# Two-level Strassen kernel on one core: DVE takes the sums, ten more products are split, two small constants are recorded later

## The chip, the cores and the metric

The kernel runs on 1 core of one Trainium2 chip. The metric is the device time of one execution in microseconds. Of the engines, PE is the matrix engine (PEld its weight load), DVE the vector engine, ACT the scalar engine, POOL the GpSimd engine, and SP the queue that issues most of the DMA transfers. Engines run their own instruction streams in order and wait for each other by semaphores.

## The reference

```python
x = x + einsum('bnr,bor->bno', einsum('bni,bri->bnr', x, B0[ids0]), A0[ids0])   # rank-16 adapter by request
base   = einsum('btd,od->bto', x, W)
logits = einsum('btd,ed->bte', x, Wr) + 5.0 * one_hot(ids1, 8)[:, None, :]
topw, topi = top_k(logits, 2); gates = sum(one_hot(topi, 8) * softmax(topw)[..., None], axis=-2)
h = einsum('btd,erd->bter', x, A1)
x = x + base + 2.0 * einsum('bter,bte,eor->bto', h, gates, B1)                  # 8 experts of rank 16
```

x is 64 x 64 x 1024 in float32, so 4096 tokens of 1024; W is 1024 x 1024. All of it is float32.

## The kernel before

The tokens lie transposed and are cut into 8 blocks of 512. Each block's first part (`early`) turns the gathered rows of the first adapter on PE (`turn`, tile pt, from a tile gb that POOL gathers by an indirect DMA), projects x by them (`project`, tile pb<-x,bt), and adds the adapter's output to x (`adapt`, tile px). The second part (`late`) computes the router's logits and the 128 expert rows (`rows`, tile ph), the gates by a chain of small DVE instructions (`gates`), and turns the gated rows on PE (`weigh`, tile pg). Two blocks make one of 4 super-blocks.

The large matrix product, W with the identity added times x, is done by super-block in two nested levels of a 7-product scheme (Strassen's in Winograd's form). The outer level makes 7 outer products (order 1, 2, 6, 7, 5, 3, 4), each on sums of quarters of W and of the tokens. Inside each, 7 inner products are made from smaller quarters, again in the order 1, 2, 6, 7, 5, 3, 4. An inner product multiplies a 128 x 512 weight tile (tag s) with a 128 x 512 token tile (ti, or a view of x or t) into PSUM tiles pa and pb: 4 matmuls that are 256 columns wide, and 2 more for the expert part's bias rows where there is one. Super-block 0 makes the sums of the weights and stores them to DRAM (`s_kept`); the later ones load them again. Outer product 1 of super-block 0 is made whole (tile pw).

From super-block 1 on, some inner products are split by a third level (`fine_product`, tile pf): 7 matmuls that are 128 columns wide take the place of the 4. Their operands are four extra sums of the weight tile (`fine_weights`, tile sf, made in super-block 1, kept in `f_kept`, loaded later) and four of the token tile (`begin_fine`, tile tt). The first four matmuls fill PSUM, and the last three, interleaved with other products, add to it, while ACT copies the half-done parts out (tile cp) and later instructions add them to the result. Which products are split is set by `fine_of`: product 2 of every outer product, and product 4 of those in `FOURTH`.

Vector work between the levels: `token_sum` (t), `inner_tokens` (ti), `outer` and `weights` (s, by `combine`), the evictions from PSUM with an addition (`leave`) and the sums of outputs (`done`). In super-block 0 `inner_tokens` is DVE's, later POOL's; the sums in `weights`, `fine_weights`, `begin_fine` and the additions of cp (`rest_`) are POOL's.

The order is not that of the source. Every step is handed to `Plan.add` with the engines it may run on, their cost in us, what it reads and writes, the pool slots it takes and a due time `at`. `Plan.order` simulates the engines with these costs: it picks the engine that can start first, and on it the step with the earliest due time among those that can start within 0.2 us. An argument `behind` holds a step back until another has begun in the plan. The instructions are then recorded in the planned order, and a scheduling layer adds the semaphores. `PACE` slows two steps that the plan puts on DVE and POOL at the same time. `SET` is when the engines are ready at the start. Every instruction is recorded through the helper at line 29, so all have one line in the profile and are told apart by their tiles. The mask that the projection's result is multiplied with, and a float copy of the experts' order, are made on DVE in front of the plan (lines 311 and 312).

Of the kernel before, what the change touches and what calls it, by code (L numbers as in the profile page):

```python
# [14 lines left out]
P = 128  # L15
# [18 lines left out]
class Plan:  # L34
# [15 lines left out]
    PACE = {"DVE": 0.36, "POOL": 0.73}  # L50
    SET = {"SP": 1.2, "DVE": 3.1, "POOL": 2.9}
# [13 lines left out]
    def order(self):  # L65
# [35 lines left out]
        clock, end, where, now = dict(self.SET), {}, {}, {}  # L101
        moved = 0.0
# [5 lines left out]
        def start(n, e):  # L108
# [20 lines left out]
            return t  # L129

        while ready:
# [8 lines left out]
            t0 = min(can[e])[0]  # L140
            _, n, t = min((steps[n]["at"], n, t) for t, n in can[e] if t <= t0 + self.LOOK)
# [3 lines left out]
            other = {"DVE": "POOL", "POOL": "DVE"}.get(e)  # L145
            if st["sb"] and other in now and clock[other] > t and steps[now[other]]["sb"]:

                mine, theirs = st["eng"][e] / self.PACE[e], (clock[other] - t) / self.PACE[other]
                both = min(mine, theirs)
                clock[e] = t + both + (mine - both) * self.PACE[e]  # L150
                clock[other] = t + both + (theirs - both) * self.PACE[other]
                end[now[other]] = clock[other]
            now[e] = n
# [28 lines left out]
def kernel(  # L182
# [74 lines left out]
    FOURTH = (1, 2, 6, 7, 3)  # L257
# [6 lines left out]
        "q": 7, "s": 27, "tt": 3, "cp": 3, "t5": 2, "t6": 2, "t7": 2, "t4": 2, "o": 3, "hg": 3, "hd": 3,  # L264
# [46 lines left out]
    dve.tensor_scalar(mask, mask, half, None, ALU.is_equal)  # L311
    dve.tensor_copy(order, order_i)
    b1_sb = const.tile([P, O], F32, name="b1_sb")

    def consts():
# [9 lines left out]

        plan.add({"POOL": 0.2}, hold, [(("gb", 0),)], [("a1",)], -56)
# [8 lines left out]
    def biases():  # L335
# [19 lines left out]
        plan.add({"DVE": 1.0}, languages, [("ids1",)] + whole(0), [("bias",)], -45)  # L355
# [47 lines left out]
    def gather(k, tag, table, at):  # L403
        def fn(e):
            made[tag, k] = new(tag, [P, D], f"{tag}_{k}")
            pool.indirect_dma_start(
                out=made[tag, k],
                out_offset=None,
                in_=table,
                in_offset=bass.IndirectOffsetOnAxis(ap=idx[:, k : k + 1], axis=0),  # L410
            )

        plan.add(
            {"POOL": 1.1}, fn, [], [((tag, k),)], at, [(tag, (tag, k))], kb=512,
            behind=[(("x", 0, 1), 0, 0)] * ((tag, k) == ("ga", 0)) + [("a1",)] * (k == 1) + [(("px", 1, 1, 0),)] * (k > 1),
        )
# [22 lines left out]
    def project(k, at):  # L439
# [29 lines left out]
        plan.add({"DVE": 0.3}, out, [(pb,)], [(bx,)], at - 8)  # L469

    def adapt(k, h, at):
# [33 lines left out]
        for gi in range(NG):  # L505
            xs = part(x, gs=[gi])
            plan.add({"DVE": 0.62}, out(gi), [(px[gi],)] + xs, xs, at - 2 + 1.5 * gi * (k == 0))
# [159 lines left out]
    f_kept = tc.dram_tile([7, 2, P, QC * QO], F32, name="f_kept")  # L667

    def fine_of(s, n):

        return ((2, 4) if n in FOURTH and (s, n) != (NSUP - 1, ORDER[-1]) else (2,)) if s >= FINE else ()
# [13 lines left out]
    DVE = {"DVE": 0.62}  # L685
    POOL = {"POOL": 1.25}

    def outer(n, at):

        if n == 5:  # L690
            m_q[5] = {k: ("m5",) + k for k in quarter[1, 0]}
            for k in m_q[5]:
                combine(m_q[5][k], quarter[1, 0][k], quarter[1, 1][k], ALU.add, at, DVE)
        elif n == 7:
            m_q[7] = quarter[1, 0]
            for k in m_q[7]:
                combine(m_q[7][k], quarter[0, 0][k], m_q[7][k], ALU.subtract, at, DVE)
        elif n == 6:
            m_q[6] = quarter[0, 0]
            for k in m_q[6]:  # L700
                combine(m_q[6][k], m_q[5][k], m_q[6][k], ALU.subtract, at, DVE)
        elif n == 3:
            m_q[3] = quarter[0, 1]
            for k in m_q[3]:
                combine(m_q[3][k], m_q[3][k], m_q[6][k], ALU.subtract, at, DVE)
# [3 lines left out]
    def weights(s, n, at):  # L709
# [17 lines left out]
        for k, (u, v, op) in {  # L727
# [8 lines left out]
            combine(out[k], uu, vv, op, at - 4, POOL)  # L736
# [9 lines left out]
    def fine_weights(s, n, k, a, at):  # L746

        t, kept = ("sf", s, n, k), f_kept[n - 1, k // 4]

        def blocks():  # L750
            made[t] = new("s", [P, QC, QO], f"sf_{s}_{n}{k}")
            return made[t].rearrange("p c (o w) -> p (c o) w", w=P)
# [5 lines left out]
        def sums(e):  # L758
            f, w4 = blocks(), made[a].rearrange("p c (o w) -> p (c o) w", w=P)
            a11, a21, a12, a22 = (w4[:, x] for x in range(4))  # L760
            v = engine[e]
            v.tensor_tensor(f[:, 0], a21, a22, ALU.add)
            v.tensor_tensor(f[:, 1], f[:, 0], a11, ALU.subtract)
            v.tensor_tensor(f[:, 2], a11, a21, ALU.subtract)
            v.tensor_tensor(f[:, 3], a12, f[:, 1], ALU.subtract)
# [4 lines left out]
        if s == FINE:  # L770
            plan.add({"POOL": 1.6}, sums, [(a,)], [(t,)], at - 3, [("s", t)], sb=True)
            plan.add({"SP": 0.1}, keep, [(t,)], [("fine", n, k)], at + 4, kb=256)
        else:
            plan.add({"SP": 0.1}, load, [("fine", n, k)], [(t,)], at - 6, [("s", t)], kb=256)
# [25 lines left out]
    def inner_tokens(s, n, m, at):  # L800
# [7 lines left out]
        for k, u, v in ((5, (0, 1), (0, 0)), (6, (1, 1), 5), (7, (1, 1), (0, 1)), (4, (1, 0), 6)):  # L808
            t = ("ti", s, n, k)

            def fn(e, t=t, k=k, u=u, v=v):
# [6 lines left out]
                POOL if s else DVE, fn, keys(*u) + vk, [(t,)], at - 5,  # L818
# [40 lines left out]
    def products(s):  # L859
# [91 lines left out]
        def leave(n, ps, i, cs, js, more=False):  # L951
# [18 lines left out]
            if d == n and not fresh:  # L970
                reads.append((name(d, i), 0, 0))
            plan.add(
                {"ACT": 0.6} if src is None else DVE, fn, reads, qk(d, i, cs, js), at() - 4,
# [5 lines left out]
        def begin_fine(n, k):  # L979
# [3 lines left out]
            def fn(e):  # L983
                made[t] = new("tt", [P, 4, P], f"tt_{s}_{n}{k}")
                f, b, v = made[t], tx(), engine[e]
                b11, b21 = b[:, 0, :P], b[:, 1, :P]
                v.tensor_tensor(
                    f[:, :2], b[:, :, P:], b[:, 0, :].rearrange("p (h t) -> p h t", t=P), ALU.subtract
                )
                v.tensor_tensor(f[:, 2], f[:, 1], b11, ALU.add)  # L990
                v.tensor_tensor(f[:, 3], b21, f[:, 2], ALU.subtract)

# [315 lines left out]
```

## Time and profile before

| | us |
|---|---|
| median of 5 runs | 515.65 |
| lowest, highest | 515.17, 517.30 |
| the profiled execution | 515.5 |
| its span | 513.7 |
| PE, PEld busy | 499.6, 440.8 |
| DVE, POOL, ACT busy | 328.5, 319.7, 71.4 |

The profile is of one execution. Busy time of an engine is the time that its instructions cover; a record of an instruction that waits for a port that another engine holds includes that wait. Each float32 matmul leaves two PE records, and successive records overlap, so what a matmul costs PE is the distance between starts. The part of the span that no engine's work explains is seen in the waits: for each engine, what it waited for and how long. The whole program reads 75.3 MB from DRAM and writes 32.8.

### The profile page before, as it was taken

The numbers are of one execution on the slowest core, as the hardware profiler recorded it, in microseconds if no ns is written. First come the engines' busy times: TensorE is split into PE (matmuls) and PEld (weight loads), VectorE is DVE, ScalarE is ACT, GpSimd is POOL, SyncE is SP. The second block draws the span as 40 slices with busy tenths as digits, with TensorE's granted clock in tenths as the row PEclk, the third lists the DMA queues.
The fourth block names the chain that finished last, engine by engine and source line by source line (L and its number), as shares of the span: only waits on it lengthen the run. The fifth ranks groups of instructions, "written<-read, shape, count | busy, mean of one in ns | idle before, by whom it ended". The sixth has DMA issues, their size and how long they took to land.

```text
span 513.7 us, 9478 instructions
## 1 busy us (share of the span) xinstructions
PE 499.6 (97%) x3648; PEld 440.8 (86%) x3648; DVE 328.5 (64%) x589; ACT 71.4 (14%) x189; POOL 319.7 (62%) x405
## 2 busy tenths in 40 slices
PE   2999999999999999999999999999999999999997
PEld 2857988888889998899888999889889899999986
DVE  0799998987965276536985456463777526742833
ACT  1111100001001130013110221102301111111110
POOL 3072058195567686997858557972954755997811
PEclk9999999999999999999999999999999999999999
DMA  8999175799576303999577644981855754581123
GB/s 275 372 362 385 66 265 214 270 326 308 178 245 215 93 2 125 330 336 352 179 237 253 218 125 127 379 273 44 286 180 181 245 154 144 166 265 41 40 98 109
DMA packets 59452, 108.69 MB, mean 212 GB/s; under 512 B 5520, under 2 KB 11664, under 8 KB 59408
## 3 DMA queue, kind: packets, MB, share of 16 engines
q1 hardware_dynamic: 57104, 99.70, 57.6%
q0 software_dynamic: 2304, 8.39, 4.8%
q8 instruction: 29, 0.48, 0.4%
q14 instruction: 15, 0.12, 0.1%
HBM read 75.30 MB, written 32.77 MB: 210 GB/s over the span
## 4 chain that ended last, share of the span: by engine, by line
PE 97%; DMA 2%; DVE 0%; issue 0%; SPq 0%; POOL 0%
PE pa L29 39%; PE pb L29 23%; PE pf L29 15%; PE ph L29 12%; PE px L29 3%; PE pw L29 3%; DMA x<-in_xT 2%; PE pt L29 1%; PE pg L29 1%; DVE o L29 0%; SPq L29 0%; DVE bx L29 0%; POOL x L29 0%
## 5 line engine op out<-in xcount | busy, mean ns | idle before, releaser
L29 PE MATMUL pa<-ti,s 128*128 128x256 f32 x432 | 102.0, 380 | 0.0
L29 PEld LDWEIGHTS pa<-ti,s 128*128 128x128 f32 x432 | 79.2, 190 | 9.8 <-issue 0.2
L29 PE MATMUL pb<-ti,s 128*128 128x256 f32 x264 | 65.6, 380 | 0.0
L29 PE MATMUL ph<-a_sb,x 128*128 128x136 f32 x512 | 62.8, 279 | 0.2 <-issue 0.2
L29 PEld LDWEIGHTS ph<-a_sb,x 128*128 128x128 f32 x512 | 61.8, 190 | 1.1 <-issue 0.4
L29 ACT COPY cp<-pf 128x128 f32<-128x128 f32 (+1 forms) x108 | 32.2, 303 | 200.8 <-PE pf L29 188.9
L29 PEld LDWEIGHTS pb<-ti,s 128*128 128x128 f32 x264 | 48.6, 190 | 5.9
L29 PE MATMUL pa<-x,s 128*128 128x256 f32 x216 | 52.4, 380 | 0.0
L29 POOL TENSOR_TENSOR ti<-x,ti 128x512 f32<-128x512 f32 x24 | 32.0, 1334 | 27.4 <-PE pf L29 22.6
L29 POOL TENSOR_TENSOR o<-o,cp 128x128 f32<-128x128 f32 (+1 forms) x54 | 34.5, 652 | 20.8 <-DVE o L29 15.6
L29 DVE TENSOR_TENSOR x<-px,x 128x512 f32<-128x512 f32 x64 | 39.8, 681 | 10.8 <-PE px L29 10.7
L29 PEld LDWEIGHTS pa<-x,s 128*128 128x128 f32 x216 | 39.4, 190 | 4.9 <-issue 0.2
L29 PE MATMUL pf<-tt,sf 128*128 128x128 f32 x216 | 42.1, 278 | 0.0
L29 POOL TENSOR_TENSOR ti<-x 128x512 f32<-128x512 f32 x24 | 31.0, 1295 | 16.7 <-PE pb L29 11.2
L29 PE MATMUL pa<-t,s 128*128 128x256 f32 x168 | 41.2, 380 | 0.0
L29 POOL TENSOR_TENSOR ti<-t 128x512 f32<-128x512 f32 x18 | 22.9, 1273 | 29.0 <-PE pa L29 16.6
L29 PEld LDWEIGHTS pf<-tt,sf 128*128 128x128 f32 x216 | 35.5, 191 | 3.2 <-issue 0.8
L29 DVE TENSOR_TENSOR o<-pa,u 128x512 f32<-128x512 f32 x32 | 22.0, 686 | 22.3 <-PE pa L29 11.2
L29 POOL TENSOR_TENSOR s<-w,w 128x512 f32<-128x512 f32 x12 | 17.2, 1429 | 29.1 <-PE pa L29 13.2
L29 POOL TENSOR_TENSOR ti<-t,ti 128x512 f32<-128x512 f32 x18 | 25.3, 1404 | 15.7 <-PE pf L29 12.1
L29 PEld LDWEIGHTS pa<-t,s 128*128 128x128 f32 x168 | 30.8, 190 | 3.9 <-issue 0.2
L29 DVE TENSOR_TENSOR o<-pb,o 128x512 f32<-128x512 f32 x35 | 23.5, 687 | 8.9 <-ACT o L29 4.6
(150 smaller groups left out, 849.4 us busy)
## 6 DMA issues: line engine op xcount, KB each, us to landing
s<-s_kept SPq DMA_DIRECT2D x147, 256.0 KB, 4.3
x<-in_xT SPq DMA_DIRECT2D x15, 1024.0 KB, 8.7
out_T<-o SPq DMA_DIRECT2D x30, 512.0 KB, 3.0
s_kept<-s SPq DMA_DIRECT2D x28, 256.0 KB, 5.1
sf<-f_kept SPq DMA_DIRECT2D x24, 256.0 KB, 3.6
s_kept<-w SPq DMA_DIRECT2D x18, 256.0 KB, 5.3
w<-in_w SPq DMA_DIRECT2D x16, 256.0 KB, 8.2
f_kept<-sf SPq DMA_DIRECT2D x12, 256.0 KB, 2.5
```

Of the source, the lines that this page charges most:

```text
L29: return self._tc.keep_in_program_order(f(*args, **kwargs))
```

## The change

`inner_tokens`, `weights` and the additions of cp (`rest_`) become DVE's alone. `rest_` is now two instructions of 256 columns, not three of 128 and 256. The sums for the split products' operands (`begin_fine`, `fine_weights`) become steps of their own, one instruction each, that the plan may put on DVE or on POOL.

`FOURTH` takes in outer products 5 and 4, and a new `THIRD` splits product 3 of outer products 3 and 4. The last outer product of the last super-block stays with product 2 alone. The eviction of a split product 3 goes to column half 1 (`js`), and pa is evicted there after product 5.

In the planner the pacing is gone. A step that touches the port that DVE and POOL share (`sb`) starts after the last such step has ended (`shared_`). DVE's costs are 0.65 for a sum and 0.69 for an eviction.

The mask and the experts' order become a planned step behind block 0's first gather. Block 2's first gather gets a POOL copy of one column ahead of it, which waits for block 1's second half of x. The weight pool has 26 slots, not 27.

```diff
-    PACE = {"DVE": 0.36, "POOL": 0.73}
-    SET = {"SP": 1.2, "DVE": 3.1, "POOL": 2.9}
+    SET = {"SP": 1.2, "DVE": 2.6, "POOL": 2.9}
...
-            return t
+
+            return (max(t, shared_), t) if st["sb"] else (t, t)
...
-            now[e] = n
+            if st["sb"]:
+                shared_ = clock[e]
...
-    FOURTH = (1, 2, 6, 7, 3)
+    FOURTH = (1, 2, 6, 7, 5, 3, 4)
+    THIRD = (3, 4)
...
-        "q": 7, "s": 27, "tt": 3, "cp": 3, "t5": 2, "t6": 2, "t7": 2, "t4": 2, "o": 3, "hg": 3, "hd": 3,
+        "q": 7, "s": 26, "tt": 3, "cp": 3, "t5": 2, "t6": 2, "t7": 2, "t4": 2, "o": 3, "hg": 3, "hd": 3,
...
-    dve.tensor_scalar(mask, mask, half, None, ALU.is_equal)
-    dve.tensor_copy(order, order_i)
...
+        def finish(e):
+            dve.tensor_scalar(mask, mask, half, None, ALU.is_equal)
+            dve.tensor_copy(order, order_i)
+
+
+        plan.add({"DVE": 0.4}, finish, [], [("mask",), ("order",)], -57, behind=[(("gb", 0),)])
...
+        held = (tag, k) == ("gb", 2)
+
+        def hold(e):
+
+            made[tag, k] = new(tag, [P, D], f"{tag}_{k}")
+            pool.tensor_copy(made[tag, k][:, :1], made["x", 1, 1][:, 0, :1])
+
+        if held:
+            plan.add(
+                {"POOL": 0.2}, hold, part(("x", 1, 1), [0]), [((tag, k),)], at, [(tag, (tag, k))]
+            )
...
-    f_kept = tc.dram_tile([7, 2, P, QC * QO], F32, name="f_kept")
+    f_kept = tc.dram_tile([7, 3, P, QC * QO], F32, name="f_kept")
...
-        return ((2, 4) if n in FOURTH and (s, n) != (NSUP - 1, ORDER[-1]) else (2,)) if s >= FINE else ()
+        if s < FINE:
+            return ()
+        if (s, n) == (NSUP - 1, ORDER[-1]):
+            return (2,)
+        return (2,) + (4,) * (n in FOURTH) + (3,) * (n in THIRD)
...
-            combine(out[k], uu, vv, op, at - 4, POOL)
+            combine(out[k], uu, vv, op, at - 4, {"DVE": 0.65})
...
-            plan.add({"POOL": 1.6}, sums, [(a,)], [(t,)], at - 3, [("s", t)], sb=True)
+            for x in range(4):
+                plan.add(
+                    {"DVE": 0.29, "POOL": 0.48}, sums(x), [(a,)] + [(t, y) for y in range(x)], [(t, x)], at - 3,
+                    [("s", t)] * (x == 0), sb=True,
+                )
...
-                POOL if s else DVE, fn, keys(*u) + vk, [(t,)], at - 5,
+                {"DVE": 0.65} if s else DVE, fn, keys(*u) + vk, [(t,)], at - 5,
...
-            plan.add({"POOL": 1.7}, fn, tk, [(t,)], at() - 3, [("tt", t)], sb=True)
+            for x, cost in enumerate(({"DVE": 0.42, "POOL": 0.75}, {"DVE": 0.29, "POOL": 0.48}, {"DVE": 0.29, "POOL": 0.48})):
+                plan.add(
+                    cost, sums(x), tk + [(t, y) for y in range(x)], [(t, x)], at() - 3,
+                    [("tt", t)] * (x == 0), sb=True,
+                )
...
-            leave(n, ps, row, ALL, (0,), True)
-            region = qk(dest[n], row, ALL, (0,))
-
-            def rest_(e):
-                o, c, v = q(dest[n], row, ALL, (0,)), made[cp], engine[e]
-                c11, c21, c2 = o[:, 0, :P], o[:, 1, :P], o[:, 1]
-                v.tensor_tensor(c11, c11, c[:, 0], ALU.add)
-                v.tensor_tensor(c2, c2, c[:, 1:3].rearrange("p h t -> p (h t)"), ALU.add)
-                v.tensor_tensor(c21, c21, c[:, 3], ALU.add)
-
-            plan.add({"POOL": 1.7}, rest_, [(cp,)] + region, region, at() - 4, sb=True)
-            done(n, row, ALL, (0,))
+            leave(n, ps, row, ALL, js, True)
+            region = qk(dest[n], row, ALL, js)
+
+            def rest_(x):
+                def fn(e):
+                    o, c, v = q(dest[n], row, ALL, js), made[cp], engine[e]
+
+                    o, c = (o[:, :, :P], c[:, 0::3]) if x == 0 else (o[:, 1].rearrange("p (h t) -> p h t", t=P), c[:, 1:3])
+                    v.tensor_tensor(o, o, c, ALU.add)
+
+                return fn
+
+            for x in range(2):
+                plan.add({"DVE": 0.42}, rest_(x), [(cp,)] + region, region, at() - 4, sb=True)
+            done(n, row, ALL, js)
...
+                if k == 5 and 3 in fine_of(s, n):
+                    leave(n, ps, 0, ALL, (1,))
...
-                    if k == 7 and 4 in fine_of(s, n):
-                        going.append([n, 4, 0])
+                    if k in (6, 5) and k - 2 in fine_of(s, n):
+                        going.append([n, k - 2, 0])
                     advance()
-                if 4 in fine_of(s, n):
-                    rest = [(n, 3)]
-                    continue
+                rest = [(n, k) for k in (3, 4) if k not in fine_of(s, n)]
+                if last(n):
+                    rest = [(n, 4), (n, 3)]
+                continue
```

## The prediction

> **What bounds the kernel now.** I read the waits of TensorE first, then the chain that ended last, the table by stretches of time, and the instructions of PE in order of time.
>
> ```profile
> PE 499.6 (97%) x3648; PEld 440.8 (86%) x3648; DVE 328.5 (64%) x589; ACT 71.4 (14%) x189; POOL 319.7 (62%) x405
> ...
> PE 97%; DMA 2%; DVE 0%; issue 0%; SPq 0%; POOL 0%
> ```
>
> ```profile
> PE pt L29 <- DMA gb<-in_b,idx: 9.3, 1, 9.3
> PE pb L29 <- DMA x<-in_xT: 0.6, 1, 0.6
> PE px L29 <- DVE bx L29: 0.4, 1, 0.4
> PE ph L29 <- issue: 0.2, 1, 0.2
> ```
>
> The second fence is every wait that PE has: about 10.5 us, all before 18.3 us. After that PE runs to 510.1 us without a pause, and the last store lands at 513.7. So between 18 and 510 us only two things count: how long PE's own instructions take, and whether a helper becomes late enough to stop PE. The stretches show how near the helpers are to that (columns: busy us and instructions of PE, PEld, DVE, ACT, POOL, then clock, DMA share, GB/s):
>
> ```profile
> 20.00:150.00 130.00, 129.98 (x984) 108.07 (x983) 115.91 (x214) 11.32 (x24) 64.02 (x60) 1.00 0.77 267
> 150.00:273.00 123.00, 123.00 (x934) 110.62 (x933) 76.11 (x135) 20.10 (x56) 95.31 (x130) 1.00 0.61 212
> 273.00:396.00 123.00, 123.00 (x935) 110.72 (x934) 73.62 (x135) 20.00 (x56) 79.83 (x102) 1.00 0.62 201
> ```
>
> DVE is 89% busy from 20 to 150 us (super-block 0) and about 61% in each later super-block; PE stands still in neither, and its clock is 1.00 throughout.
>
> **The change part by part.** *1. Ten more split products.* In super-blocks 1 to 3, product 4 is now split for outer products 5 (three times) and 4 (twice; the very last outer product stays out), and product 3 for outer products 3 (three times) and 4 (twice): 10 products. A whole one is 4 matmuls 256 columns wide, a split one is 7 matmuls 128 wide; each matmul leaves two records. Bias matmuls stay as they are. What each costs PE is the distance between starts, since records overlap:
>
> ```profile
> 236.37 1.89 PE L29 MATMUL pa<-ti,s 128*128 128x256 f32 x8
> 238.10 0.39 PE L29 MATMUL pf<-tt,sf 128*128 128x128 f32 x2
> ...
> 245.04 0.61 PE L29 MATMUL pf<-x,s 128*128 128x128 f32 x4
> 245.49 0.39 PE L29 MATMUL pf<-tt,sf 128*128 128x128 f32 x2
> 245.71 0.39 PE L29 MATMUL pf<-tt,s 128*128 128x128 f32 x2
> 245.93 1.89 PE L29 MATMUL pa<-x,s 128*128 128x256 f32 x8
> ```
>
> Eight wide records take 238.10 - 236.37 = 1.73 us, 0.216 each. Eight narrow ones take 245.93 - 245.04 = 0.89, 0.111 each, a little over half. A split product is 14 x 0.111 = 1.56 against 1.73: 0.17 us saved, 1.7 us for ten. The ends are 1.6 (narrow records at 0.112) and 2.16 (exactly half, 0.108). I take 1.7.
>
> The Trainium skill, "TensorE: Matmul & The Clock Gate", section "Back-to-back issue gap", speaks against this part: it gives a sustained spacing of 81 ns at 128 columns and 131 ns at 512, because weight loads share the time. Interpolated (an estimate) that is 98 ns at 256, a split product would cost 14 x 81 - 8 x 98 = 350 ns more, and ten would lose 3.5 us. The rows above, 111 against 216 ns in this kernel's own type, decide.
>
> *2. PE's order.* Matmuls 32 rows or columns wide cost PE a changeover. Block 7's first projection (pb<-x,bt), one piece of 64 records before, stands in the changed program in two pieces with block 6's gate transposes between. All other narrow runs number the same. Price:
>
> ```profile
> 205.53 1.08 PE L29 MATMUL pb<-x,bt 128*32 128x128 f32 x32
> 206.54 0.49 PE L29 MATMUL pf<-tt,sf 128*128 128x128 f32 x2
> ...
> 247.75 1.95 PE L29 MATMUL pb<-x,bt 128*32 128x128 f32 x64
> 249.64 0.49 PE L29 MATMUL pf<-tt,sf 128*128 128x128 f32 x2
> ```
>
> Two halves are 2 x 1.01, the whole 1.89: 0.13 more; and the 256-wide row ahead of such a run lasts about 0.1 longer (245.93 to 247.75 is 1.82, not 1.73). Together +0.2 us.
>
> *3. Sums from POOL to DVE.* POOL gives up all 112 sums 512 wide (28 of weights in super-block 0, 84 of tokens), the 54 groups' additions of the split products' copies (36 groups of three), and, where the planner so chose, part of the split operands' sums. In the built program VectorE's tensor-tensor instructions go from 515 to 778, POOL's from 376 to 153. By rows of DVE's own: 112 x 0.683 = 76 us (row w<-w,w 684 ns); 92 additions of copies 256 wide (46 products, two each) x 0.424 = 39; ten more evictions of pf x 0.687 = 7; 40 sums 128 wide x 0.28 and 9 of 256 x 0.424 = 15. That is 137 us more. Against it: a DVE sum of two SBUF tiles that meets a POOL sum waits it out today (u<-u,o 1132 ns, o<-v,o 1017, against 683 undisturbed). Over all such rows that wait is about 42 us, 18 of them before 150 us. POOL's tensor work falls from about 304 to about 90 us (116 x 0.52 + 37 x 0.80), so I expect some 30 us back. DVE ends near 435 us, 85%; back to back its sums start every 0.60 us, so the page may show 400 to 440.
>
> By stage: super-block 0 gets 28 x 0.68 = 19 us and loses about 18 of lock waits: 117 of 130, 90%, as now. A later one gets 28 x 0.68 + 13 + 2 + 5 = 39 and loses about 10: 105 of 123, 86%. PE had no wait at 89%, so I price part 3 at nothing on the path, save 0.2 us for small waits at the gate transposes (pg), which need a chain of some 17 short DVE instructions that now queue among more sums. Bounds: nothing, and what rival C says. ACT gets 30 copies x 0.30 = 9 us, 16% in all: no bound.
>
> *4. The start.* The mask and the order are recorded later, but in the built program DVE's first seven instructions stand in the same order, with nothing between:
>
> ```profile
> 2.37 0.23 DVE L29 TENSOR_SCALAR idx<-ids_sb,rcol 128x8 int32<-128x8 int32 x1 [0.78 <-DMA ids_sb<-in_ids]
> 2.51 0.28 DVE L29 TENSOR_SCALAR mask<-mask,half 128x128 f32<-128x128 f32 x1
> 2.71 0.17 DVE L29 CAST order<-order_i 128x32 f32<-128x32 int32 x1
> 2.89 1.11 POOL L29 DMA_INDIRECT gb<-in_b,idx  x1 [1.11 <-DVE order L29]
> ```
>
> The gather waits for idx, not for the order, by the program; yet it starts as the order ends. Nothing in front of it changes, so the start stays: 0. If the gather did move up to idx's end, it would gain 0.29 us, but PE next waits for x (0.6 us), so at most 0.3; a loss of the same size is as possible.
>
> *5. The later gathers.* Block 2's b0 gather gets a POOL copy in front (0.18 us as its like at 4.93) that waits for block 1's second half of x. Queued behind on POOL is only block 3's gather and then work of super-block 1. Before, eight POOL sums of 1.3 us stood ahead of it (28.1 to 38.3) and it issued at 38.5; now it follows block 1's adapter matmuls, near 41 to 43. Landing takes 6.6 us, PE needs it at 61: hidden by over 10 us. If that cover went, PE would wait what is missing.
>
> *6. DMA and slots.* Four more 256 KB writes and six more reads through SP: 2.6 MB at a mean share of 61% after 150 us. The weight pool has 26 slots, not 27, and an outer product takes 7 plus 2.3, not 1.7: 2.8 outer products of 17.6 us ahead against a landing of 4.3. Cost 0; each load that came late would cost up to that 4.3.
>
> *7. The end.* The last eviction (0.42 us) still follows PE's last matmul. But two pieces of the last outer product change places, and the last stores (256, 256, 128, 128 KB) come within some 1.5 us: 128 KB ahead of the last, at the 350 GB/s of the busy stretches, is up to 0.37 us. I take 0.2; ends 0 and 0.4.
>
> **Sum.** -1.7 + 0.2 + 0.2 + 0.2 = -1.1 us. The profiled run took 515.5 us (span 513.7), 0.15 under the median of 515.65, so 514.4 on its own scale and 514.5 on the median's. 0.3%, about what a measurement of this kernel tells from no change, is 1.55 us: below 514.1 is faster.
>
> **Rivals.** *A, the forecast:* 0.48. *B, nothing is lost:* no changeover, tail or wait costs, and narrow matmuls run nearer to half: -1.6 to -2.2 us, 513.3 to 514.1. For it: PE has no wait after 18 us even at DVE's 89%. Against: the piece in two is in the program. 0.32. *C, DVE becomes the bound at the gates:* pg of blocks 1 to 7 waits for its chain of short DVE instructions behind sums. For it: 86% leaves 18 us free in 123, and one sum in front of a link costs 0.68. Against: super-block 0 ran so. At 0.7 us each, 7 times is 4.9 us: -1.3 + 4.9, 519 us; it is slower than before by over 0.3% from (1.1 + 1.55) / 7 = 0.4 us at each. 0.2. *The change doesn't do what it says* holds for part 4, with no time in it.
>
> The range of 513.4 to 518.2 takes in most of B and the lower half of C; A's own is 514.1 to 515.6. Faster 0.32, within 0.3% 0.48, slower 0.20.
>
> **What will show it.** Right: PE's waits still end at 18 us, PE's busy time falls by 1.3 to 1.7, DVE is 78 to 87% busy, POOL under 25%, the groups u<-u,o and o<-v,o near 0.7 us. Wrong: a row "PE pg <- DVE" or "PE pa <- DVE" of over a microsecond (C); narrow pf records more than 0.112 apart; weights late on DMA; a gather that PE waits for near 61 us.

## The result, and the profile after

The changed kernel takes 516.7 us (median of 34 runs, 514.73 to 518.46) beside 515.95 us for the kernel before (57 runs, 515.13 to 517.3): a ratio of 1.0014, 95% interval 1.0008 to 1.002. The forecast was 514.5 us, 1.1 us under the 515.65 us that the kernel before had shown by then; the changed kernel came out about 0.7 us, 0.15%, slower than the kernel before: inside the range of the prediction, and on the wrong side of the time before. Its profiled run took 516.49 us, with a span of 514.7 us.

The first two lines are the busy times and the chain that ended last, of the changed kernel:

```profile
PE 499.1 (97%) x3708; PEld 442.0 (86%) x3708; DVE 423.0 (82%) x852; ACT 79.9 (16%) x219; POOL 111.5 (22%) x183
...
PE 89%; DMA 7%; DVE 3%; issue 0%; SPq 0%; POOL 0%; DVEq 0%
```

The chain was PE's alone before (97%); now DMA has 7% of it and DVE 3%. These are all waits of PE in the same run:

```profile
PE pt L29 <- DMA gb<-in_b,idx: 9.5, 1, 9.5
PE pb L29 <- DMA x<-in_xT: 0.6, 3, 0.2
PE pa L29 <- DVE o L29: 0.5, 1, 0.5
PE px L29 <- DVE bx L29: 0.4, 1, 0.4
PE ph L29 <- issue: 0.2, 1, 0.2
```

Before, PE waited for x once, at the start; now two of the three waits for x lie after 20 us, and the wait of bank pa for DVE is new. The stretches (busy us and instructions of PE, PEld, DVE, ACT, POOL, then clock, DMA share, GB/s) show DVE where the prediction had it, and no stretch in which it is full:

```profile
20.00:150.00 130.00, 129.81 (x1000) 108.76 (x999) 114.41 (x238) 11.73 (x25) 16.99 (x27) 1.00 0.73 256
150.00:273.00 123.00, 122.91 (x940) 110.76 (x940) 101.88 (x206) 20.85 (x60) 44.01 (x76) 1.00 0.67 221
273.00:396.00 123.00, 122.78 (x953) 110.78 (x952) 108.57 (x214) 24.01 (x69) 26.86 (x38) 1.00 0.66 216
```

PE's own work did shrink. In order of time, instructions of PE in super-block 1:

```profile
244.56 1.89 PE L29 MATMUL pa<-x,s 128*128 128x256 f32 x8
246.29 0.38 PE L29 MATMUL pf<-tt,sf 128*128 128x128 f32 x2
246.51 0.61 PE L29 MATMUL pf<-x,s 128*128 128x128 f32 x4
246.96 0.39 PE L29 MATMUL pf<-tt,sf 128*128 128x128 f32 x2
247.18 0.39 PE L29 MATMUL pf<-tt,s 128*128 128x128 f32 x2
247.40 0.39 PE L29 MATMUL pf<-ti,sf 128*128 128x128 f32 x2
```

Eight wide records take 246.29 - 244.56 = 1.73 us and eight narrow ones 247.40 - 246.51 = 0.89, as before the change. PE now has 80 records of 256 columns fewer and 140 of 128 columns more. At 0.216 and 0.112 us that is 1.6 us less: the forecast's 1.7 us are there, at 1.6. Something else gives them back and more.

**Where it goes back: loads of x.** The second half of a block's x has to find a free slot among seven. Before, that of block 4 was issued with the first half at 200 us, and that of block 6 at 321 us (DMA issues of SP in the kernel before; two loads in the first line):

```profile
199.57 0.94 SPq L29 DMA_DIRECT2D x<-in_xT  x2
...
321.45 0.38 SPq L29 DMA_DIRECT2D x<-in_xT  x1
```

In the changed kernel:

```profile
210.32 0.38 SPq L29 DMA_DIRECT2D x<-in_xT  x1
...
333.48 0.38 SPq L29 DMA_DIRECT2D x<-in_xT  x1
```

Ten and twelve microseconds later. PE projects these halves at 209.6 and 330.4 us before and at 216.0 and 339.3 us after: a lead of 9 us has become 5.7 and 5.8, for a load of 1 MB. The slot explains the lateness. Before, DVE had done the difference x <- x,x of super-block 1, which gives a slot of block 2 back, by 199.6 us (last of these instructions of DVE, kernel before):

```profile
198.96 0.68 DVE L29 TENSOR_TENSOR x<-x,x 128x512 f32<-128x512 f32 x1
```

In the changed kernel DVE is behind with it:

```profile
206.12 1.28 DVE L29 TENSOR_TENSOR x<-x,x 128x512 f32<-128x512 f32 x2
212.89 1.60 DVE L29 TENSOR_TENSOR x<-x,x 128x512 f32<-128x512 f32 x2
```

so the written order gives the load another slot, that of a token sum t, which PE reads last here:

```profile
208.40 1.89 PE L29 MATMUL pa<-t,s 128*128 128x256 f32 x8
```

That product ends at 210.29, and the load is issued at 210.32. The slot that the difference gives back comes free at 214.5 us and goes to block 5's first half, issued at 214.51. Nobody waits for DVE in this; DVE's lateness travels through a slot to SP, and through a landing to PE.

The wait for x at 99.92 us is not of this kind. Its load was issued at 92.78 us, 7.1 us ahead of its use; the same load had 7.0 us before the change (88.15 for 95.20 us) and caused no wait. Here the landing itself took longer.

**The end.** An eviction on DVE waits for a store of o to give a slot back, and PE's bank pa waits for that eviction. In the kernel before:

```profile
485.85 2.42 SPq L29 DMA_DIRECT2D out_T<-o  x2
...
488.70 0.69 DVE L29 TENSOR_TENSOR o<-pa,u 128x512 f32<-128x512 f32 x1 [0.86 <-DMA out_T<-o]
```

In the changed kernel (SP, then DVE, then PE):

```profile
487.98 1.72 SPq L29 DMA_DIRECT2D out_T<-o  x2
...
492.65 0.69 DVE L29 TENSOR_TENSOR o<-pa,u 128x512 f32<-128x512 f32 x1 [1.32 <-DMA out_T<-o]
...
492.56 0.38 PE L29 MATMUL pf<-tt,sf 128*128 128x128 f32 x2
493.40 0.92 PE L29 MATMUL pa<-ti,s 128*128 128x256 f32 x3 [0.45 <-DVE o L29]
```

Such a wait existed before and cost PE nothing. Now the store goes out 2.1 us later, and the slot comes free at about 492.6 us, 4.6 us after the issue. Before, it came 2.8 us after the issue. The first of the two stores is the one that the eviction waits for, by its semaphore. A transfer raises its semaphore in 16 steps, and the trace records them: 15 had come by 490.79 us, ahead of 491.33, when DVE was ready; the last came at 492.63. During this store a 16 KB load of instructions, part of the program itself, ran (DMA queue q8, 489.13 us, 1.5 us long). In six profiles such a load falls into this store (changed, e0, e14, e9, e1, e3), and in each the last step comes 1.8 to 2.3 us after the 15th; in the other profiles none falls into it, and the last step comes within 0.04 us. The two go together; that the one makes the other was not tried apart.

The last two rows also show what a wait costs. Two narrow records take 0.22 us, so PE could have started pa at 492.78 and started at 493.40: 0.62 us lost, where the idle time is 0.45. The records overlap, so each wait costs 0.16 us more than the idle time shown. Counted so, PE lost 0.35, 0.25 and 0.38 us to the waits for x at 99.92, 216.03 and 339.28 us, 1.0 us in all.

From PE's last matmul to the end of the span, 3.6 us have become 4.4 (510.35 to 514.72). The last stores before the change, five in 5.17 us, and after it, four in 2.01:

```profile
505.80 5.17 SPq L29 DMA_DIRECT2D out_T<-o  x5
```

```profile
509.41 2.01 SPq L29 DMA_DIRECT2D out_T<-o  x4
```

### The profile page after: what moved, and what is told of

Read it like the earlier page. It is cut to its first block, busy times and chain, and to the rows that moved or that the text cites. A ratio compares the mean times of both kernels' runs of the same rounds, so it can differ in the third digit from the quotient of the medians.

```text
span 514.7 us, 9697 instructions
## 1 busy us (share of the span) xinstructions
PE 499.1 (97%) x3708; PEld 442.0 (86%) x3708; DVE 423.0 (82%) x852; ACT 79.9 (16%) x219; POOL 111.5 (22%) x183
## 4 chain that ended last, share of the span: by engine, by line
PE 89%; DMA 7%; DVE 3%; issue 0%; SPq 0%; POOL 0%; DVEq 0%
PE pa L29 34%; PE pb L29 18%; PE pf L29 17%; PE ph L29 12%; DMA x<-in_xT 6%; PE px L29 3%; PE pw L29 3%; PE pt L29 1%; DVE o L29 1%; DMA out_T<-o 1%; PE pg L29 1%; DVE ti L29 1%; DVE u L29 1%; DVE s L29 0%; SPq L29 0%
## 5 line engine op out<-in xcount | busy, mean ns | idle before, releaser
L29 ACT COPY cp<-pf 128x256 f32<-128x256 f32 (+1 forms) x138 | 41.0, 303 | 194.5 <-PE pf L29 192.9
L29 PE MATMUL pb<-ti,s 128*128 128x256 f32 x224 | 55.8, 380 | 0.0
L29 PE MATMUL pf<-tt,sf 128*128 128x128 f32 x276 | 52.2, 277 | 0.0
L29 PEld LDWEIGHTS pf<-tt,sf 128*128 128x128 f32 x276 | 45.6, 191 | 4.0 <-issue 0.4
L29 POOL TENSOR_TENSOR tt<-x 128x256 f32<-128x256 f32 x14 | 11.8, 840 | 113.0 <-DMA s_kept<-s 45.5
L29 PEld LDWEIGHTS pa<-t,s 128*128 128x128 f32 x152 | 27.7, 190 | 3.2
L29 DVE TENSOR_TENSOR o<-o,cp 128x256 f32<-128x256 f32 x56 | 25.0, 449 | 3.0
L29 POOL TENSOR_TENSOR sf<-s 128x128 f32<-128x128 f32 x31 | 16.7, 540 | 39.7 <-PE pa L29 18.2
L29 DVE TENSOR_TENSOR o<-pf,o 128x512 f32<-128x512 f32 x28 | 19.2, 685 | 7.2 <-PE pf L29 7.1
L29 DVE TENSOR_TENSOR ti<-x,ti 128x512 f32<-128x512 f32 x30 | 22.2, 741 | 1.0 <-PE pb L29 0.5
L29 DVE TENSOR_TENSOR ti<-t 128x512 f32<-128x512 f32 x24 | 17.6, 734 | 6.5 <-PE pb L29 5.7
```

The source lines that it names most:

```text
L29: return self._tc.keep_in_program_order(f(*args, **kwargs))
```

## The experiments

All on one core. The theory, S: the change loses through transfers that start too late for want of a slot, and through a crowded end. Rivals: L, DVE's load as such costs PE, wherever the transfers stand; N, the loss is scatter of the start. The table gathers what the profiles and times show; "x" and "pa" are PE's idle times in waits for x and for the bank pa after 20 us, "tail" is the time from PE's last matmul to the span's end, all in us.

| run | time (before beside it) | ratio, 95% | x | pa | tail |
|---|---|---|---|---|---|
| before | 515.95 | | 0 | 0 | 3.6 |
| changed | 516.7 (515.95) | 1.0014 (1.0008-1.002) | 0.4 | 0.5 | 4.4 |
| e0 changed again | 517.1 (516.16) | 1.0019 (1.0001-1.0037) | 1.9 | 0.6 | 4.4 |
| e14 changed again | 517.02 (515.9) | 1.0018 (0.9999-1.0038) | 1.4 | 0.5 | 4.4 |
| e1 token sum early | 515.86 (516.16) | 0.9998 (0.9985-1.001) | 1.1 | 0.9 | 4.1 |
| e2 8 slots | 515.85 (516.16) | 0.9996 (0.9977-1.0014) | 0 | 0 | 4.4 |
| e13 8 slots again | 515.38 (515.9) | 0.9988 (0.9972-1.0004) | 0 | 0 | 4.4 |
| e3 4 slots for o | 515.71 (516.16) | 0.9997 (0.9983-1.0011) | 0.7 | 0 | 3.8 |
| e4 changed, preload | 525.6 (516.13) | 1.0153 (1.0103-1.0203) | 6.8 | 0 | 4.0 |
| e5 before, preload | 521.43 (516.13) | 1.0091 (1.0059-1.0124) | 4.1 | 0 | 3.5 |
| e6 no new splits | 516.78 (516.13) | 1.002 (0.9998-1.0041) | 0 | 0 | 3.6 |
| e10 8 slots, no new splits | 515.62 (515.88) | 0.999 (0.9979-1.0) | 0 | 0 | 3.6 |
| e12 one product whole | 515.82 (515.9) | 1.0007 (0.9983-1.0032) | 0 | 0 | 3.9 |
| e7 8 slots, one whole | 514.91 (516.13) | 0.9971 (0.9953-0.999) | 0 | 0 | 4.0 |
| e11 the same again | 514.9 (515.88) | 0.9981 (0.9965-0.9998) | 0.8 | 0 | 4.0 |
| e8 splits, sums on POOL | 520.62 (515.88) | 1.0091 (1.0061-1.0121) | 0.3 | 0.6 | 4.4 |
| e9 parts 4, 5 back | 516.7 (515.88) | 1.0007 (0.9992-1.0022) | 1.6 | 0.9 | 4.4 |

Idle times under 0.15 us don't show in these sums. With 12 runs a ratio is good to some 0.15%, 0.8 us, about the size of what is looked for: no single row decides by its time alone, but the waits and the issue times in the profiles are plain. The 0.8 us of e11 lies at 27.7 us, in block 1's first load, which no edit touches.

**e0 and e14: the changed kernel again.** No edit.

> The changed kernel once more, unedited, as the standard for the others on this chip and to see which parts of its +1.0 us against the kernel before come again in a second profile. Theory S (slots): the loss sits in transfers that start too late for want of a slot: waits of PE for x near 99.9, 216 and 339 us (0.26, 0.16, 0.29 us), a wait of PE's bank pa near 493 us (0.6 us) and a tail of about 4.4 us from PE's last matmul to the last store; all of these come again, and the ratio to the kernel before is 1.001 to 1.002. Theory N (nothing but scatter at the start): these waits differ from profile to profile, and the 0.35 us by which PE's first matmul began later is what the ratio is made of.

> The changed kernel a third time, as the standard on this chip: 0.6 to 1.1 us over the kernel before, waits of PE for x near 100, 216 and 340 us, a wait for pa near 494 us and a tail of 4.4 us.

The ratio came again (1.0019 and 1.0018), and the waits at the same places, only larger. Waits of PE after 20 us in e0:

```profile
PE pb L29 <- DMA x<-in_xT: 1.9, 2, 1.1
PE pa L29 <- DVE o L29: 0.6, 1, 0.6
```

The loads are issued as in the first profile (210.6 and 333.7 us), yet the wait near 340 us is 1.1 us in place of 0.2, 1.2 in e14 and 1.6 in e9. For the load waited for near 340 us the last of the 16 semaphore steps is what varies: it came 1.1, 1.3 and 1.6 us after the 15th in e0, e14 and e9, and 0.2 us after it in the first profile. So a load without lead is paid as its landing happens to turn out, and the first profile was a lucky one. The first matmul starts at 9.54, 9.27 and 9.13 us in the three profiles (9.27 before, 8.8 to 9.8 over all runs), with the same program in front of it: the 0.3 us that it lost in the first was scatter. N falls as the cause: in e0 and e14 the first matmul is no later than before, and the loss is there.

**e1: the token sum earlier.**

```diff
+        for st in done:
+            x = st["writes"][0][0] if st["writes"] else ""
+            if isinstance(x, tuple) and x[0] == "x" and x[1] in (3, 5) and x[2] == 0:
+                if any(k[0] == ("x", x[1] - 1, 0) for k in st["reads"]):
+                    st["start"] = max([st["start"] - 8] + [steps[d]["start"] + 0.01 for d in st["dep"]])
         return sorted(done, key=lambda st: st["start"])
```

> Only the place of 8 instructions changes: the difference x <- x,x of super-blocks 1 and 2 (token sum 1) is recorded up to 8 us earlier in DVE's stream, so the slot that the second half of blocks 4 and 6 loads into comes free earlier. Theory S: these two loads are issued about 2.4 and 1.3 us earlier than 210.3 and 333.5 us, the waits of PE for x at 216 and 339 us (0.45 us together) go, the time falls by 0.3 to 0.5 us against the changed kernel; the wait at 99.9 us, the one near 493 us and the tail of 4.4 us stay. Theory L (DVE's load as such costs PE, wherever the loads stand): no change of the time.

The two loads were issued at 208.31 and 331.75 us, 2.0 and 1.7 us earlier. The wait at 216 us is gone. The one near 340 us is not (0.5 us, with 7.5 us of lead), and the expectation missed there: a lead of 7.5 us is not always enough. The time fell by 1.2 us against e0, more than the traced waits explain, and less than the two intervals together can assure.

**e2 and e13: one slot more for x.**

```diff
-        "q": 7, "s": 26, "tt": 3, "cp": 3, "t5": 2, "t6": 2, "t7": 2, "t4": 2, "o": 3, "hg": 3, "hd": 3,
+        "q": 8, "s": 23, "tt": 3, "cp": 3, "t5": 2, "t6": 2, "t7": 2, "t4": 2, "o": 3, "hg": 3, "hd": 3,
```

> One slot more for x and token sums (8 instead of 7), paid with three weight slots (23 instead of 26); no instruction is added or taken away. Theory S: the second halves of blocks 4 and 6 are issued some 13 us earlier (near 196 and 321 us), the waits of PE for x at 216 and 339 us are gone, the scatter of the runs shrinks from 3.7 us towards the 2.2 us of the kernel before, and the time falls by 0.4 to 0.7 us against the changed kernel. The wait near 493 us and the tail stay. A cost would show as PE waiting for weights (s or sf) on DMA. Theory L: no change, or slower by the fewer weight slots.

> All ten splits with 8 slots for x once more (it had 515.85 us on the first chip, three of its twelve runs near 518). Theory S: under the changed kernel by 0.7 to 1.2 us on this chip, with the tail still 4.4 us, and above the version that also leaves one product whole by 0.4 to 0.9 us. If the slots are worth nothing: the time of the changed kernel.

No wait of PE for x or pa is left after 20 us in either profile; the two loads are issued at 195.67 and 319.76 us in e13. The time falls by 1.2 us against e0 and by 1.6 against e14, each on the same chip. No load of weights is late at 23 slots, and DVE is as busy as ever:

```profile
PE 499.0 (97%) x3708; PEld 442.8 (86%) x3708; DVE 421.3 (82%) x848; ACT 79.5 (15%) x219; POOL 114.1 (22%) x187
```

421 us where the changed kernel has 423: L, in which the load itself costs, falls. Two points missed: the scatter of the runs did not shrink (514.40 to 518.26 in e2), and the wait for pa near 493 us went too, although o has its 3 slots as before. The profiles tell why. These are the landings (last number, us) of the awaited store in e0, issued at 489.06 us, and in e2, issued at 487.93:

```profile
out_T<-o SPq DMA_DIRECT2D x1, 512.0 KB, 4.8
```

```profile
out_T<-o SPq DMA_DIRECT2D x1, 512.0 KB, 2.8
```

In e2 it is issued as late as in the changed kernel and lands 2 us sooner; the load of instructions falls behind it, at 492.96 us. So the wait for pa went with the place of that load and not with the slot for x. The 1.2 and 1.6 us are the worth of both.

**e3: one slot more for o.**

```diff
-        "q": 7, "s": 26, "tt": 3, "cp": 3, "t5": 2, "t6": 2, "t7": 2, "t4": 2, "o": 3, "hg": 3, "hd": 3,
+        "q": 7, "s": 25, "tt": 3, "cp": 3, "t5": 2, "t6": 2, "t7": 2, "t4": 2, "o": 4, "hg": 3, "hd": 3,
```

> One slot more for the outer products' results (o 4 instead of 3), paid with one weight slot (25). Theory S: DVE no longer waits for the store of o at 491.3 us, PE's wait for the bank pa near 493 us (0.6 us) goes, the last stores are spread as before and the tail falls from about 4.4 to about 3.6 us: together 1.2 to 1.4 us less than the changed kernel, below the kernel before by 0.3 to 0.6 us. The wait for x at 216 us stays, that at 339 us may go too, since the load is issued some 2 us earlier. Theory L: the wait at 493 us is DVE being late with sums, not with the store, and stays with the tail: no change.

As expected: no wait of DVE for the store, none of pa for DVE, a tail of 3.8 us, and the waits for x still there (0.7 us). The store itself still takes 4.7 us to land; with a fourth slot nobody waits for it. 1.4 us under e0.

**e4 and e5: a small load in front, in both kernels.** A first quarter of the same data is loaded to the same place ahead of the load proper; the result is unchanged.

```diff
+            if (k, i) in ((4, 1), (6, 1)):
+                sp.dma_start(made[t][:, 0], xT[i * HC * P : (i * HC + 1) * P, k * TB : (k + 1) * TB])
             sp.dma_start(
```

> The changed kernel with one extra load of 256 KB (the first quarter of the same data, into the same place) in front of the second half of blocks 4 and 6; the loads proper wait for it. That puts each of the two about 2.4 to 3 us later. Theory S: these loads have no cover left in the changed kernel, so the delay comes out at PE nearly whole: waits of PE for x near 217 and 341 us of about 2.5 us each in place of 0.16 and 0.29, and the run is 4.5 to 6 us longer than the changed kernel (521 to 523 us). Theory L: transfers have cover, DVE's load is what counts: below 1 us more.

> The kernel before with the same extra load in front of the same two transfers. Theory S: there the second halves of blocks 4 and 6 were issued about 9 us ahead of PE's use (200.1 for 209.6 us, 321.5 for 330.4 us), against a landing of 5.5 to 6 us, so 3 us of cover are left and the delay of 2.4 to 3 us is hidden: PE shows no wait for x after 20 us of more than 0.5 us, and the time rises by 0 to 1 us. Were the price the same as in the changed kernel (4.5 to 6 us), the lead would not be what differs between the two.

Both cost more than expected, and e5's expectation failed as it stands: the kernel before pays 5.3 us. The profiles tell why. In e5 the load proper is issued 5.7 us after the small one (200.93 and 206.67 us) and 4.6 us the second time (326.28 and 330.92), not 2.4 to 3, which I put down to a 1 MB load issued 0.5 and 3.7 us in front of the small one (that was not tried apart). Of these 5.7 and 4.6 us PE pays 2.4 and 1.7 (waits of PE in e5):

```profile
212.90 0.87 PE L29 MATMUL pb<-x,bt 128*32 128x128 f32 x12 [2.37 <-DMA x<-in_xT]
...
336.98 0.75 PE L29 MATMUL pb<-x,bt 128*32 128x128 f32 x20 [1.73 <-DMA x<-in_xT]
```

so 3.4 and 2.9 us were cover. In e4 the delays are 2.9 us (210.83 to 213.71) and 3.2 (339.80 to 343.03), and PE pays all of them:

```profile
219.43 1.94 PE L29 MATMUL pb<-x,bt 128*32 128x128 f32 x32 [2.98 <-DMA x<-in_xT]
...
348.53 1.29 PE L29 MATMUL pb<-x,bt 128*32 128x128 f32 x20 [3.15 <-DMA x<-in_xT]
```

Cover: none. This pair, with one profile of each, measures what S claims: about 3 us of cover for these two loads in the kernel before, and 0 in the changed one. The rest of the price is the clock (last section).

**e6 and e10: without the ten new splits**, with 7 and with 8 slots for x (e10 has e2's slots too).

```diff
-    FOURTH = (1, 2, 6, 7, 5, 3, 4)
-    THIRD = (3, 4)
+    FOURTH = (1, 2, 6, 7, 3)
+    THIRD = ()
```

> The changed kernel without its ten more split products (the fourth products of outer products 5 and 4 and the third products of 3 and 4 stay whole); the sums stay with DVE. Theory S: PE has 1.7 us more of its own work, but DVE has some 26 us less, so the load of block 6's second half is issued near 322 us and not 333.5, the store of o is not late, the waits near 339 and 493 us (0.3 to 1.1 and 0.6 to 0.8 us) go and the tail is 3.6 and not 4.4 us: the time is within 0.5 us of the changed kernel, so the splits pay nothing net. As the prediction had it (splits worth 1.7 us and nothing lost to them): 1.7 us slower than the changed kernel, 518.4 us beside 516.7.

> No ten new splits, and one slot more for x (8, with 23 for weights): with the run without splits and 7 slots, the one with splits and 8, and the changed kernel this makes a table of two by two. Theory S: here the slots have nothing to cure but the small waits near 99.5, 215.6 and 332 us (0.5 us), so it stands 0 to 0.5 us under the run without splits (516.8), at 516.3 to 516.8, and the ten splits on top of 8 slots are worth 1.0 to 1.6 us, while on 7 slots they were worth nothing. PE's own time differs by the forecast 1.6 us. Theory L: the splits are worth the same with either number of slots.

On 7 slots the splits pay nothing: 516.78 us without, 516.7 to 517.1 with. In e6 the load of block 6 goes out at 322.19 us, the store of o that matters at 485.05 and the tail is 3.6 us. On 8 slots the expected 1.0 to 1.6 us didn't show in the time either: 515.62 us without, 515.38 and 515.85 with. PE's stretch from first to last matmul is 1.4 us shorter with them (500.07 us in e2, 501.43 in e10), and the tail takes 0.8 back; the other 0.6 us are within what these runs can tell. One more point missed: e10 was to stand 0 to 0.5 us under e6 and stands 1.2 under it, on another chip, so the eighth slot for x was worth about as much without the splits as with them. In e6 three waits for x, at 99.50, 215.64 and 332.31 us, are each too short to show as idle time; by the distances between starts they cost 0.8 us. That e10 stands level with the kernel before (0.999, interval 0.9979 to 1.0) says that the sums on DVE cost nothing that these runs can tell once x has its slot.

**e7, e11 and e12: one product left whole**, with 8 slots and with 7 (e12).

```diff
-        return (2,) + (4,) * (n in FOURTH) + (3,) * (n in THIRD)
+        return (2,) + (4,) * (n in FOURTH) + (3,) * (n in THIRD and (s, n) != (NSUP - 1, 3))
```

> One slot more for x (8, with 23 weight slots) and the last super-block's third product of outer product 3 left whole, which takes some 2.7 us of sums from DVE before the end. Theory S: no wait of PE for x at 216 and 339 us, none near 493 us, stores at the end spread as in the kernel before and the tail at 3.6 to 3.8 instead of 4.4 us: 1.2 to 1.6 us under the changed kernel, 0.5 to 0.8 us under the kernel before (near 515.4 us where before is 516.0). Theory L: no better than the changed kernel, and 0.2 us worse for the product left whole.

> The version with 8 slots for x and one product left whole once more, on another chip, to narrow its interval. Theory S: again 0.8 to 1.4 us under the kernel before, no wait of PE for x or for DVE of more than 0.15 us after 20 us, and a tail of 3.9 to 4.0 us. If the first result was scatter: a ratio of 0.999 to 1.001.

> The changed kernel with 7 slots for x as it is, and only the last super-block's third product of outer product 3 left whole. Theory S, in its parts: the waits of PE for x near 100, 216 and 340 us (0.7 to 2.4 us together in the profiles so far) stay; the tail falls from 4.4 to 3.9 us because the last stores no longer come within 1.6 us, and the wait for the bank pa near 494 us (0.6 to 1.1 us) goes: 0.6 to 1.3 us under the changed kernel on this chip. If the end is worth nothing: the time of the changed kernel, and the 8 slots alone made the gain of the version with both.

e12 is 1.2 us under e14 on the same chip, with the wait for pa gone and the last stores spread again. By its time alone this is not clear of the scatter (514.44 to 521.23 us). No load of instructions falls into the awaited store here either, and it lands 2.8 us after its issue, so this run can't say that the product left whole ended the wait for pa. The last stores:

```profile
504.47 5.93 SPq L29 DMA_DIRECT2D out_T<-o  x5
```

Its waits for x were also under what shows in this profile, though the loads go out as late as ever (333.39 us): scatter again. With both edits the time is 514.9 us on two chips, under the kernel before both times (0.9971 and 0.9981, both intervals below 1). e7 was expected only 0.5 to 0.8 us under the kernel before; it is 1.2 under it. This is the version that beats both: nine of the ten splits, 8 slots for x, 23 for weights.

**e8: the splits without the move of the sums.** The kernel before with the splits and their places in PE's order as in the change; the sums stay POOL's.

```diff
-    FOURTH = (1, 2, 6, 7, 3)
+    FOURTH = (1, 2, 6, 7, 5, 3, 4)
+    THIRD = (3, 4)
...
-                    if k == 7 and 4 in fine_of(s, n):
-                        going.append([n, 4, 0])
+                    if k in (6, 5) and k - 2 in fine_of(s, n):
+                        going.append([n, k - 2, 0])
                     advance()
```

> The kernel before with the ten more split products alone: all sums stay where they were (POOL makes them, 1.7 us for the operands and 1.7 us for the copies of each), slots as before. Theory S: the splits' 1.6 us of PE's time come out only if the helpers keep up; POOL goes from 62% to about 68% and must wait for DVE and DVE for it, so its late sums stop PE: slower than the kernel before by 2 to 8 us, with waits of PE on POOL or DVE in super-blocks 1 to 3. That would say that the move of the sums to DVE is what lets the splits be there at all. Rival (the move only costs): the splits alone gain 1 to 1.6 us on the kernel before.

4.7 us slower than the kernel before. Waits of PE after 20 us:

```profile
PE pf L29 <- ACT cp L29: 1.1, 3, 0.4
PE pf L29 <- DVE x L29: 0.8, 1, 0.8
PE pa L29 <- DVE o L29: 0.6, 1, 0.6
PE pb L29 <- DMA x<-in_xT: 0.3, 1, 0.3
PE pa L29 <- PE pf L29: 0.2, 1, 0.2
```

3.0 us, and a tail of 4.4. These and the 1.6 us saved don't add up to the whole 4.7 us; the rest is not in waits that show. The move to DVE doesn't only cost: with the sums left on POOL, in this plan, the splits lose far more than they save.

**e9: parts 4 and 5 undone.**

```diff
+    dve.tensor_scalar(mask, mask, half, None, ALU.is_equal)
+    dve.tensor_copy(order, order_i)
     b1_sb = const.tile([P, O], F32, name="b1_sb")
...
-        held = (tag, k) == ("gb", 2)
+        held = False
```

> The changed kernel with the mask and the experts' order written ahead of the plan again and block 2's first gather without the copy that holds it back. As the prediction had it (both cost nothing): the gather of block 0 is issued at 2.9 us right behind the order, PE's first matmul starts between 9.2 and 9.7 us as in the other profiles, and the time is that of the changed kernel within 0.4 us. Rival N (the start is what lost): the first matmul 0.3 us earlier, and the time 0.3 us less.

516.7 us, as the changed kernel. The gather is issued at 2.92 us in both. PE's first matmul came at 8.82 us, by an early landing of that gather (8.7 for 9.4 us); the time didn't follow.

## Why the forecast was wrong

*1, the splits:* right. 1.6 us were measured for the forecast 1.7, one of its two ends. The rule weighed against the rows, "Back-to-back issue gap" of the Trainium skill's "TensorE: Matmul & The Clock Gate", would have made this a loss of 3.5 us by the prediction's estimate; the rows of after show 0.111 and 0.216 us again.

*2, PE's order:* right, 0.1 for 0.2 us (the 32-wide runs of pb take 13.74 us in place of 13.60).

*3, the sums:* the load was forecast well. DVE has 423 us where 400 to 440 were given, 114 of 130 us in the first stretch (117), 102 and 109 of 123 in the next two (105); POOL is at 22%. The sums that met POOL's are back, in the changed kernel:

```profile
L29 DVE TENSOR_TENSOR o<-v,o 128x512 f32<-128x512 f32 x16 | 11.5, 718 | 0.5
...
L29 DVE TENSOR_TENSOR u<-u,o 128x512 f32<-128x512 f32 x16 | 11.2, 698 | 0.0
```

(1017 and 1132 ns before). The gate transposes cost nothing that shows, so rival C did not happen. But "I price part 3 at nothing on the path" holds only for PE's direct waits on DVE. The step looked at who reads DVE's results and not at who gets a slot back from DVE.

*6, "DMA and slots ... Cost 0":* this is the step that failed. It counted the weight slots, for which no wait shows even at 23, and left out the other two pools whose slots DVE's work helps to give back: x, 7 slots, and o, 3. Their price, by four profiles of the same loads and stores (changed, e0, e14, e9): idle times of PE for x of 0.4, 1.9, 1.4 and 1.6 us, and for pa of 0.5 to 0.9. By the distances between starts, which also catch the short waits, PE lost 1.0, 2.4, 2.0 and 2.1 us for x, 1.9 in the mean, and 0.6 to 1.0 for pa, 0.8 in the mean. Some 0.4 of the 1.9 belong to the load near 100 us, whose lead had not changed.

*7, the end:* the mechanism was right, its size not: 0.8 us for the 0.2 taken and the 0.4 given as an end. The four last stores came within 1.6 us, as said. The last store takes 3.70 us from its issue to the span's end in place of 3.11 (511.02 to 514.72, and 510.62 to 513.73). Where the trace has its landing, it lands 2.13 us after its issue in e0 and 1.76 in e10, whose stores are spread: the crowd costs 0.37, just what the mean rate gave as the end. What the step left out is the rest: the last store is issued 0.2 us later behind PE's last matmul, and from its landing to the span's end, while SP goes through the other stores, 1.6 us pass in place of 1.3.

*4 and 5:* right, as far as e9 can tell, and by an unchanged order of the first rows (after):

```profile
2.39 0.23 DVE L29 TENSOR_SCALAR idx<-ids_sb,rcol 128x8 int32<-128x8 int32 x1 [0.80 <-DMA ids_sb<-in_ids]
...
2.91 1.11 POOL L29 DMA_INDIRECT gb<-in_b,idx  x1 [1.14 <-DVE order L29]
```

**The sum with measured terms:** -1.6 + 0.1 + 1.9 + 0.8 + 0.8 = +2.0 us. The spans of the four profiled runs are 1.8 us longer in the mean than that of the kernel before (515.5 and 513.7 us), which the sum explains. The medians say only +0.7 to +1.1: the four profiled runs lie 0.4 us above their medians in the mean, and the profiled run before lies 0.45 under its own. Which wait is shorter in the runs without a profile, no run shows. That the waits for x and the end are causes and not only beside the loss is shown by e2 and e13, and by e3, each of which takes two of the terms away and comes down by 1.2 to 1.6 us; how much of this is the waits for x, how much the wait for pa and how much the tail, the times can't part.

That the time stayed inside the range was luck: the forecast gain was there, and a loss that the prediction had at nothing outweighed it by a little. Its list of what would show it wrong named "a row PE pa <- DVE of over a microsecond" and weights late on DMA. What came was such a row of 0.5 to 0.9 us, and x late on DMA by 0.2 to 1.6 us, at three places.

## What to carry to other kernels

Before giving an engine more work off the critical path, list not only who reads its results but which buffers it is the last to read, and what load or store next takes each of them: the lead of that load is the true cover, issue time to use against its landing time. A lead equal to the landing looks free in one profile and is paid in the next, so take the cover from a lead in hand and not from the absence of a wait. The last part of a transfer can come 1 to 2 us after the rest, as here, and a lead has to cover that too. A few slots moved from a pool that has too many (23 weight slots did for 26) to the one that is short went with a gain of 1.2 and 1.6 us, about what the ten products save PE.

## What was not expected of the hardware

A long pause costs PE twice. In e4 PE stood for 2.98 us and then ran at half its granted clock for some 6 us (stretches as above):

```profile
216.00:219.60 3.60, 0.62 (x7) 0.25 (x9) 0.69 (x1) 0.00 (x0) 2.50 (x6) 0.88 0.97 358
219.60:222.00 2.40, 2.40 (x35) 2.02 (x31) 0.57 (x2) 0.00 (x0) 0.00 (x0) 0.50 1.05 404
222.00:224.00 2.00, 2.00 (x7) 1.64 (x7) 0.41 (x2) 0.00 (x0) 0.00 (x0) 0.50 1.04 385
224.00:226.00 2.00, 2.00 (x8) 1.68 (x7) 1.20 (x2) 0.27 (x1) 0.66 (x1) 0.61 0.69 260
```

With clocks of 0.50, 0.50 and 0.61, these 6.4 us hold 3.0 us less work; the second pause, 3.15 us, lost another 1.6. Waits of 6.8 us for the 0.4 to 1.9 without the small loads, 4.6 us of clock, and some 1.0 us less for pa and the tail add up to 8.5 to 10 us; e4 is 8.9 us over the changed kernel. In e5 a pause of 2.37 us halved the clock, one of 1.73 us did not:

```profile
213.00:215.00 2.00, 2.00 (x33) 1.62 (x33) 0.11 (x1) 0.00 (x0) 0.00 (x0) 0.50 1.06 408
...
337.00:339.00 2.00, 2.00 (x41) 1.80 (x42) 0.29 (x1) 0.27 (x1) 1.28 (x2) 1.00 1.06 408
```

The Trainium skill, "TensorE: Matmul & The Clock Gate", section "Part 1: The HAM clock gate (the "warmup" mystery)", has the clock fall to half after an idle window of about 3.4 us that runs freely of the kernel. The half is what the rows show; here it fell after pauses of 2.4 us and 3.0 us already. In the changed kernel itself no wait after 20 us is longer than 1.6 us in any profile, and the clock stays at 1.00: the waits there have no such second price.
